# Picking the source of each list place by an exclusive or and a minimum, with the positions added on TensorE

## The chip, the cores and the metric

The kernel runs on one core of one Trainium2 chip. The metric is the device time of one execution in microseconds (us). Three executions of the kernel before took 1736.59, 1736.99 and 1740.82 us.

## The reference

Two layers of graph attention, each followed by a residual and a layer norm, over 3327 nodes with 1024 features. The adjacency is sparse: an edge is drawn with probability 0.0024 in each direction, and every node has its own loop. Cut to what matters:

```python
# layer 0: 8 heads of 128
h = (x @ W).reshape(C, H, D)
e = leaky(alpha_src[:, :, None] + alpha_dst[:, None, :])   # leaky slope 0.2
e = where(adj == 0, -inf, e)
out = softmax(e, -1) @ h
x = layernorm(x + out)
# layer 1: one head of 1024, features after the sum
h = x @ W1
e = leaky(h @ a1 + (h @ a2).T)
x = layernorm(x + relu(softmax(where(adj > 0, e, neg), 1) @ h))
```

## The kernel before

The nodes are cut into 26 tiles of 128 rows (`NT`). The kernel has two arms, by pairs for a dense graph and by lists for a sparse one; these inputs take the lists. It runs in three stages.

**Projection and listing (about the first 580 us).** TensorE multiplies the 26 tiles of x by W0 in fp32 (`together`, L573), with the score columns appended. ScalarE moves the products out (`keep`, L585 to L589), and they are stored as a table of rows `h0_d`. Beside that, a generator `listing` turns the rows of the adjacency into lists of sources, one tile after the other. For each tile:

- `words` (L413, L418) counts ones and packs the mask; `keys` and `columns` (L320, L322, L429 to L444) extract, for every row, up to 32 neighbours as numbers source+1 in a row of `KMAX` = 32 places, `pack`.
- `places` (L462 to L468) writes this list into a moving matrix `mv` in two bf16 parts (high and remainder) and makes a 0/1 matrix `place`, which says for each of 17 x 128 slots to which target row it belongs. `spread` (L474) makes four masked copies of `mv`, one for each group of 32 targets.
- `give` (L486, L493) multiplies `place` by the copies, so that every slot receives its target's list, offset and factors in PSUM. It has three parts (n = 0, 1, 2): the first two hold list, offset and factors, the third only the last bits of the 8 factors (columns `XR:XL`). There are four blocks for the four groups and one of single rows (`EB`).
- `take` (L505 to L512) copies the result out of PSUM on ScalarE.
- `sources` (L520 to L534) picks on VectorE, for each slot, the list entry that it wants: the wanted position is the slot's number less the list's offset, `kq`; a compare of the 32 positions with `kq`, a product with the list and a sum leave source+1, or 0 where the slot is empty. From that comes `idx`, an integer: the row to gather, or a number out of bounds (`NONE`), or row 0 for the four tiles in `FIRST`.

The order on every engine is fixed when the program is built: `pace` is called after every two steps of a projection, and moves `listing`, `counting` and, from tile 13 on, `sums_so_far` ahead by set amounts. `sums_so_far` already gathers rows of `h0_d` by indirect DMAs from GpSimd's queue (L691), weights them on VectorE (L708 to L712) and sums them on TensorE (L721). In VectorE's queue, `sources` of one tile stands right before `places` of the next, and so before its `spread` on ScalarE and its `give` on TensorE.

**Layer 0 by lists (about 581 to 1040 us).** Indirect DMAs gather rows of `h0_d` by `idx` (L1077); VectorE makes weights (L1152 to L1155), TensorE sums (L1178), and the new rows go to `y_d`.

**Layer 1 by lists (about 1040 to 1735 us).** Gathers from `y_d` (L1077), sums (L1278), then the product with W1 (L1310).

`idx` of the last tile ends the first stage: the flag that chooses the arm is read after it, and GpSimd's first instruction of the next stage, L1022, follows it.

Of the kernel before, what the change touches and what calls it, by code (L numbers as in the profile page):

```python
# [12 lines left out]
I32 = mybir.dt.int32  # L13
AF = mybir.ActivationFunctionType
OP = mybir.AluOpType
AX = mybir.AxisListType
# [3 lines left out]
P = 128  # L20
SLOPE = 0.2
EPS = 1e-5
NONE = 1 << 20
# [3 lines left out]
def kernel(  # L27
# [29 lines left out]
    nc = tc.nc  # L57
    N, D = x.shape
    H, DH = a0_src.shape
# [9 lines left out]
    KMAX = 32  # L69
    GT = 32  # L70
    NG = P // GT
    EB = 4
    NB = NG * EB + 1
# [13 lines left out]
    HB = EB // 2  # L87
# [3 lines left out]
    FIRST = 0, 1, EARLY, EARLY + 1  # L91
    XN, XR, XL = 1, 2, 2 + H
    XB = XL + KMAX
    NX, XE = XB + 1, XB + 1
    NY = XE + 2
    XS = 256
    RING = 8
    chunks = [(c, min(CT, NT - c)) for c in range(0, NT, CT)]
    assert NT % 2 == 0 and D == 2 * HALF and DH == P and H * DH == D and w1.shape[1] == D
# [31 lines left out]
    idx = const.tile([P, NT, NB], I32, name="idx")  # L131
# [49 lines left out]
    class Phase:  # L181
# [16 lines left out]
        def sbuf(self, tag, shape, bufs, name=None, dt=F32):  # L198
            return self.pool.tile(shape, dt, tag=tag, name=name or tag, bufs=bufs)
# [66 lines left out]
        def edge_constants(self):  # L266
            self.io_w = self.iota([P, WD], [[1, WD]], "io_w")

            self.io_q = self.iota([P, HG2], [[2 * P, HB], [2, P // 8], [P // 4, 8]], "io_q", base=1)
            self.io_e = self.iota([P, P], [[2, P // 8], [P // 4, 8]], "io_e", base=1)  # L270
            for g in range(1, NG, 2):
                r = slice(g * GT, (g + 1) * GT)
                nc.gpsimd.tensor_scalar(self.io_q[r, :P], self.io_q[r, :P], float(2 * P), None, op0=OP.add)
                nc.gpsimd.tensor_scalar(self.io_q[r, P:], self.io_q[r, P:], float(-2 * P), None, op0=OP.add)
            self.own_g = self.pool.tile([P, NG], F32, bufs=1, name="own_g")
            nc.vector.memset(self.own_g, 0.0)
            for g in range(NG):
                nc.vector.memset(self.own_g[g * GT : (g + 1) * GT, g : g + 1], 1.0)
            part = self.pool.tile([P, 3, NB], I32, bufs=1, name="part")
            nc.gpsimd.iota(part[:, 0, NB - 1 :], pattern=[[0, 1]], base=0, channel_multiplier=1)  # L280
            for b in range(EB):
                for g in range(NG):
                    nc.gpsimd.iota(
                        part[:, 0, b * NG + g : b * NG + g + 1], pattern=[[0, 1]], base=(b + g) % HB * P,
                        channel_multiplier=1,
                    )
            nc.vector.tensor_scalar(
                part[:, 1, :], part[:, 0, :], 7, 4, op0=OP.bitwise_and, op1=OP.logical_shift_left
            )
            nc.vector.tensor_scalar(  # L290
                part[:, 2, :], part[:, 0, :], 3, 15, op0=OP.logical_shift_right, op1=OP.bitwise_and
            )

            nums = self.pool.tile([P, 1], I32, bufs=1, name="nums")
            nc.vector.tensor_scalar(nums, part[:, 0, NB - 1 :], GT - 1, None, op0=OP.bitwise_and)
            self.mvs = self.pool.tile([P, RING, 3, NY], BF16, bufs=1, name="mvs")
            nc.vector.memset(self.mvs, 0.0)
            for c, of in ((XN, nums), (NY - 1, part[:, 0, NB - 1 :])):
                nc.vector.tensor_scalar(
                    self.mvs[:, :, 0, c : c + 1], of.unsqueeze(1).to_broadcast([P, RING, 1]), 1.0, None, op0=OP.add  # L300
                )
            self.places = self.pool.tile([P, RING, 14], F32, bufs=1, name="places")
            self.degrees = self.pool.tile([P, NT, 2], BF16, bufs=1, name="degrees")
            nc.vector.tensor_scalar(part[:, 0, :], part[:, 0, :], -P, None, op0=OP.bitwise_and)
            for n in range(2):
                nc.vector.tensor_tensor(part[:, 0, :], part[:, 0, :], part[:, n + 1, :], OP.bitwise_or)
            self.io_k = self.pool.tile([P, NB], F32, bufs=1, name="io_k")
            nc.vector.tensor_copy(self.io_k, part[:, 0, :])
            self.io_l = self.iota([P, KMAX], [[1, KMAX]], "io_l")
            self.bit = self.pool.tile([P, 8, KMAX], I32, bufs=1, name="bit")  # L310
            self.base = self.pool.tile([P, 8, KMAX], F32, bufs=1, name="base")
            for b in range(8):
                first = (b & 1) * NP // 2 + (b >> 1 & 1) * NP // 4 + (b >> 2) * NP // 8 + 1
                nc.vector.memset(self.bit[:, b, :], 512 << b)
                nc.vector.memset(self.base[:, b, :], float(first))
# [60 lines left out]
    class Edges:  # L376
# [101 lines left out]
        def give(self, b):  # L478

            if b == 0:  # L480
                self.xp = self.ph.xp
            for n in range(3):
                if b == EB:
                    s = slice(XR, XL) if n == 2 else slice(XR, NY)
                    at = NG * NX - XR
                    nc.tensor.matmul(  # L486
                        self.xp[:, EB - 1, at + s.start : at + s.stop], self.place[:, b * P :], self.mv[:, n, s],
                        start=n == 0, stop=n == 2,
                    )
                    continue  # L490
                s = slice(XR, XL) if n == 2 else slice(b // HB, b // HB + XB)
                to = self.xp[:, b, : NG * NX].rearrange("p (g c) -> p g c", g=NG)
                nc.tensor.matmul(  # L493
                    to[:, :, s], self.place[:, b * P : (b + 1) * P], self.mvg[:, :, n, s], start=n == 0, stop=n == 2
                )

        def take(self):
            sbuf = self.ph.sbuf
            self.xs = sbuf("xs", [P, NB, KMAX + 3], 1)
            re = sbuf("re", [P, NB, H], 2)  # L500
            m = NB - 1
            xb = self.xp[:, :, : NG * NX].rearrange("p b (g c) -> p b g c", g=NG)
            xe = self.xp[:, EB - 1, NG * NX :]
            lists = self.xs[:, :m, :].rearrange("p (b g) c -> p b g c", g=NG)
            nc.scalar.activation(lists[:, :, :, 1 : KMAX + 1], xb[:, :, :, XL:XB], AF.Copy)  # L505
            nc.scalar.activation(lists[:, :HB, :, 0], xb[:, :HB, :, 0], AF.Copy)
            nc.scalar.activation(lists[:, HB:, :, 0], xb[:, HB:, :, XB], AF.Copy)
            nc.scalar.activation(self.xs[:, m, 1:], xe[:, H : H + KMAX + 2], AF.Copy)
            nc.scalar.activation(re[:, :m, :].rearrange("p (b g) h -> p b g h", g=NG), xb[:, :, :, XR:XL], AF.Copy)
            nc.scalar.activation(re[:, m, :], xe[:, :H], AF.Copy)  # L510
            nc.scalar.activation(tgt[:, self.t, :m].rearrange("p (b g) -> p b g", g=NG), xb[:, :, :, XN], AF.Copy)
            nc.scalar.activation(tgt[:, self.t, m:], xe[:, NY - 1 - XR : NY - XR], AF.Copy)  # L512
            nc.sync.dma_start(re_d[self.t], re)

        def sources(self):

            sbuf, ph, t = self.ph.sbuf, self.ph, self.t
            xv, m = self.xs, NB - 1
            kq = sbuf("kq", [P, NB], 1)
            nc.vector.tensor_tensor(kq[:, :m], ph.io_k[:, :m], xv[:, :m, 0], OP.subtract)  # L520
            nc.vector.tensor_tensor(kq[:, m:], ph.io_k[:, m:], xv[:, m, KMAX + 2 :], OP.subtract)
            eq = sbuf("eq", [P, NB, KMAX], 1)
            nc.vector.tensor_tensor(
                eq, ph.io_l.unsqueeze(1).to_broadcast([P, NB, KMAX]),
                kq.unsqueeze(2).to_broadcast([P, NB, KMAX]), OP.is_equal,
            )
            nc.vector.tensor_tensor(eq, eq, xv[:, :, 1 : KMAX + 1], OP.mult)
            v = sbuf("v", [P, 2, NB], 1)
            nc.vector.tensor_reduce(v[:, 0, :], eq, AX.X, OP.add)

            nc.vector.tensor_scalar(
                v[:, 1, :], v[:, 0, :], 0.0, float(1 if t in FIRST else NONE), op0=OP.is_equal, op1=OP.mult
            )
            nc.vector.scalar_tensor_tensor(idx[:, t, :], v[:, 0, :], -1.0, v[:, 1, :], op0=OP.add, op1=OP.add)  # L534


    with ExitStack() as own, tc.manual_schedule():
        ph = Phase(own, "proj", {"A": 3})
# [9 lines left out]
        lists = []  # L548
# [373 lines left out]
        for t in range(3, NT):  # L922
# [3 lines left out]
            if t == 5:  # L926
                n, own_a = NT - 1, pool.tile([P, NT], I32, bufs=1, name="own")
                nc.vector.memset(own_a[:, n:], 0)
                step, m = adj.ap[0][0] + 1, rows(n)
# [660 lines left out]
```

## Time and profile before

| what | value |
|---|---|
| executions | 1736.59, 1736.99, 1740.82 us (median 1736.99) |
| the profiled execution's own time | 1737.93 us |
| its span in the profile | 1735.9 us |
| mean granted TensorE clock | 0.923 |
| PE busy | 1461.5 us, 84% |
| DVE (VectorE) busy | 1159.6 us, 67% |
| POOL (GpSimd) busy | 1053.2 us, 61% |
| ACT (ScalarE) busy | 472.7 us, 27% |

The busy shares are means over three stages that differ. They don't say which engine sets the time of the first stage, where the change lies; for that, a table of the busy time in stretches of the span and the waits of each engine in such a stretch are needed. A wait is named by what came last before the waiting instruction.

### The profile page before, as it was taken

The numbers are of one execution on the slowest core, as the hardware profiler recorded it, in microseconds if no ns is written. First come the engines' busy times: TensorE is split into PE (matmuls) and PEld (weight loads), VectorE is DVE, ScalarE is ACT, GpSimd is POOL, SyncE is SP. The second block draws the span as 40 slices with busy tenths as digits, with TensorE's granted clock in tenths as the row PEclk, the third lists the DMA queues.
The fourth block names the chain that finished last, engine by engine and source line by source line (L and its number), as shares of the span: only waits on it lengthen the run. The fifth ranks groups of instructions, "written<-read, shape, count | busy, mean of one in ns | idle before, by whom it ended". The sixth has DMA issues, their size and how long they took to land.

```text
span 1735.9 us, 33973 instructions
## 1 busy us (share of the span) xinstructions
PE 1461.5 (84%) x12635; PEld 840.6 (48%) x12635; DVE 1159.6 (67%) x3132; ACT 472.7 (27%) x1370; POOL 1053.2 (61%) x1311
## 2 busy tenths in 40 slices
PE   9799979889988576567666644999999999999998
PEld 5566655555655355455444432344444444444443
DVE  6699999899997698686877855354444444444443
ACT  5677763333333212222222122110111111110110
POOL 5433245666566576565657666677767776676650
PEclk9899999999999788887888887899999999999999
DMA  7699998999999999999999999999999999999980
GB/s 187 113 166 171 183 247 316 354 399 397 379 361 341 333 409 410 400 399 381 404 389 385 378 387 380 358 399 401 393 395 392 396 392 392 388 393 410 386 332 37
DMA packets 190321, 595.96 MB, mean 343 GB/s; under 512 B 37914, under 2 KB 47924, under 8 KB 190146
## 3 DMA queue, kind: packets, MB, share of 16 engines
q0 software_dynamic: 131056, 459.23, 73.6%
q1 hardware_dynamic: 56052, 123.63, 19.3%
q10 hardware_dynamic: 3038, 10.83, 1.7%
q8 instruction: 102, 1.67, 0.4%
q14 instruction: 73, 0.60, 0.1%
HBM read 593.53 MB, written 54.99 MB: 374 GB/s over the span
## 4 chain that ended last, share of the span: by engine, by line
PE 40%; DMA 12%; DVE 8%; issue 4%; POOL 1%; ACT 0%; DVEq 0%; SPq 0%; ACTq 0%; POOLq 0%
PE mm L1310 22%; PE acc L1278 13%; DMA src<-h_d,idx 4%; DMA near<-h_d,idx 3%; PE acc L1178 3%; DVE e L1155 2%; DMA src<-y_d,idx 1%; DVE y L1195 1%; PE tr L205 1%; DMA own<-h_d 1%; DVE pr L1043 1%; DVE st L226 1%; DMA near<-y_d,idx 1%; DVE y L233 1%; PE acc L1167 1%
## 5 line engine op out<-in xcount | busy, mean ns | idle before, releaser
L573 PE MATMUL mm<-wt,xT 128*128 128x384 f32 (+1 forms) x1248 | 414.3, 477 | 0.5 <-DMA xT<-in_x_t_dram 0.5
L1310 PE MATMUL mm<-wt,xT 128*128 128x512 f32 x832 | 387.6, 605 | 0.0
L1077 POOL DMA_INDIRECT src<-y_d,idx x248 | 252.6, 1019 | 118.9 <-PE acc L1278 43.2
L573 PEld LDWEIGHTS mm<-wt,xT 128*128 128x128 f32 x1248 | 230.3, 194 | 128.3 <-issue 33.5
L1313 DVE SCALAR_TENSOR_TENSOR o<-mm,y 128x512 f32<-128x512 f32 x52 | 36.0, 692 | 315.6 <-PE mm L1310 315.6
L1310 PEld LDWEIGHTS mm<-wt,xT 128*128 128x128 f32 x832 | 149.9, 189 | 198.4 <-issue 193.5
L1077 POOL DMA_INDIRECT src<-h_d,idx x152 | 163.8, 1077 | 86.4 <-PE acc L1178 26.7
L1077 POOL DMA_INDIRECT near<-y_d,idx x168 | 170.5, 1015 | 66.0 <-PE acc L1278 18.2
L691 POOL DMA_INDIRECT near<-h_d,idx x112 | 121.9, 1088 | 65.0 <-PE part L721 36.3
L1178 PE MATMUL acc<-src,e 128*32 128x129 f32 x2432 | 100.7, 333 | 70.8 <-DVE e L1155 70.8
L1278 PE MATMUL acc<-src,es 128*32 128x341 f32 x1488 | 123.2, 465 | 24.3 <-DVE es L1269 24.3
L1077 POOL DMA_INDIRECT near<-h_d,idx x96 | 103.4, 1077 | 61.9 <-PE acc L1178 15.8
L1178 PEld LDWEIGHTS acc<-src,e 128*32 128x32 f32 x2432 | 84.3, 134 | 88.7 <-DVE e L1155 77.6
L1292 ACT ACTIVATE z<-y,ri 128x342 f32<-128x342 f32 (+1 forms) x78 | 39.5, 570 | 298.3 <-DVE ri L1288 298.3
L1178 PE MATMUL acc<-near,e 128*32 128x129 f32 x1664 | 70.9, 340 | 56.1 <-DVE e L1155 45.2
L1155 DVE TENSOR_TENSOR e<-oh,way 128x1024 f32<-128x1024 f32 x90 | 109.9, 1221 | 9.1 <-PE acc L1178 1.0
L208 ACT ACTIVATE xT<-tr 128x512 f32<-128x512 f32 x52 | 31.1, 597 | 236.0 <-PE tr L205 236.0
L1167 PE MATMUL acc<-own,ident 128*128 128x387 f32 (+1 forms) x156 | 70.4, 561 | 29.3 <-ACT own L1137 25.2
L1178 PEld LDWEIGHTS acc<-near,e 128*32 128x32 f32 x1664 | 59.7, 138 | 69.4 <-DVE e L1155 48.7
L1278 PEld LDWEIGHTS acc<-src,es 128*32 128x32 f32 x1488 | 42.7, 111 | 93.7 <-issue 43.0
L413 ACT ACTIVATE junk<-ad 128x1664 uint8<-128x1664 uint8 x52 | 83.0, 1597 | 7.0 <-POOL ad L402 5.4
L1278 PE MATMUL acc<-near,es 128*32 128x342 f32 (+1 forms) x1008 | 82.9, 462 | 2.0 <-DVE es L1269 2.0
(232 smaller groups left out, 2311.1 us busy)
## 6 DMA issues: line engine op xcount, KB each, us to landing
y_d<-y SPq DMA_DIRECT2D x26, 514.0 KB
y<-y_d SPq DMA_DIRECT2D x26, 514.0 KB
xT<-in_x_t_dram SPq DMA_DIRECT2D x26, 512.0 KB
h_d<-ht SPq DMA_DIRECT2D x25, 524.0 KB
y<-in_x_dram SPq DMA_DIRECT2D x25, 512.0 KB
out_dram<-o SPq DMA_DIRECT2D x25, 512.0 KB
ad<-in_adj_dram POOLq DMA_DIRECT2D x25, 415.9 KB
own<-half_d SPq DMA_DIRECT2D x20, 516.0 KB
```

Source lines behind the costliest of these rows:

```text
L208: nc.scalar.activation(part, tr, AF.Copy)
L413: nc.scalar.activation(junk, ad[:, n * THR : (n + 1) * THR], AF.Copy, accum_out=self.d[:, n : n + 1])
L573: nc.tensor.matmul(accs[t, c], xT[t][:, k, :], wt[:, k, CUTS0[c] : CUTS0[c + 1]], start=k == 0, stop=k == KT - 1)
L691: nc.gpsimd.indirect_dma_start(out=src[n % 3][:, g, :], out_offset=None, in_=h0_d[:THR, :], in_offset=bass.IndirectOffsetOnAxis(ap=idx[:, ...
L1077: nc.gpsimd.indirect_dma_start(out=s[:, g, :w], out_offset=None, in_=table[:n, :], in_offset=bass.IndirectOffsetOnAxis(ap=idx[:, t, b * NG ...
L1155: nc.vector.tensor_tensor(e, oh.unsqueeze(2).to_broadcast([P, ng, H, wide]), wp.unsqueeze(3).to_broadcast([P, ng, H, wide]), OP.mult,)
L1167: nc.tensor.matmul(self.acc[n].rearrange("p h d -> p (h d)"), ident, part, start=False, stop=False)
L1178: nc.tensor.matmul(self.acc[h // 3][g * GT : (g + 1) * GT, h % 3, :], e[:, g, h, :], rowsof[:, g, h, :], start=j == 0 and h in HEADS, stop ...
L1278: nc.tensor.matmul(self.acc[c][to, :m], es[:, g, :], s[:, g, CUTS[c] : CUTS[c + 1]], start=b == 0, stop=b == EB,)
L1292: nc.scalar.activation(z[:, cut], self.res[:, cut], AF.Copy, scale=ri[:, 1:2])
L1310: nc.tensor.matmul(acc, xT[:, k, :], wt1[:, k, half], start=k == 0, stop=k == KT - 1)
L1313: nc.vector.scalar_tensor_tensor(o[:, half], acc, 0.0, res[:, half], op0=OP.max, op1=OP.add)
```

## The change

The entries of a list get their position added: entry number l arrives as source+1 plus 4096 l (`STEP` = 4096). TensorE adds it, as the third part of the split: `mv`'s third part holds the 32 numbers 4096 l in the columns of the list, written once for all eight buffers, and the third matmul of every block covers 40 columns of each group in place of 8. `take` writes the lists as int32 in a tile of their own and the offsets in a second one (five copies in place of four). `sources` forms 4096 `kq` as int32, takes the exclusive or of the list with it, which leaves a number under 4096 only at the wanted entry, and takes the minimum over the 32 places.

```diff
+    STEP = 1 << 12
...
-            self.io_l = self.iota([P, KMAX], [[1, KMAX]], "io_l")
+            io_l = self.iota([P, KMAX], [[STEP, KMAX]], "io_l")
+            nc.vector.tensor_copy(self.mvs[:, :, 2, XL:XB], io_l.unsqueeze(1).to_broadcast([P, RING, KMAX]))
...
-                    s = slice(XR, XL) if n == 2 else slice(XR, NY)
+                    s = slice(XR, XB) if n == 2 else slice(XR, NY)
...
-                s = slice(XR, XL) if n == 2 else slice(b // HB, b // HB + XB)
+                s = slice(XR, XB) if n == 2 else slice(b // HB, b // HB + XB)
...
-            self.xs = sbuf("xs", [P, NB, KMAX + 3], 1)
+            self.xs, self.xo = sbuf("xs", [P, NB, KMAX], 1, dt=I32), sbuf("xo", [P, NB], 1)
...
-            nc.scalar.activation(lists[:, :, :, 1 : KMAX + 1], xb[:, :, :, XL:XB], AF.Copy)
-            nc.scalar.activation(lists[:, :HB, :, 0], xb[:, :HB, :, 0], AF.Copy)
-            nc.scalar.activation(lists[:, HB:, :, 0], xb[:, HB:, :, XB], AF.Copy)
-            nc.scalar.activation(self.xs[:, m, 1:], xe[:, H : H + KMAX + 2], AF.Copy)
+            offs = self.xo[:, :m].rearrange("p (b g) -> p b g", g=NG)
+            nc.scalar.activation(lists, xb[:, :, :, XL:XB], AF.Copy)
+            nc.scalar.activation(self.xs[:, m, :], xe[:, H : H + KMAX], AF.Copy)
+            nc.scalar.activation(offs[:, :HB, :], xb[:, :HB, :, 0], AF.Copy)
+            nc.scalar.activation(offs[:, HB:, :], xb[:, HB:, :, XB], AF.Copy)
+            nc.scalar.activation(self.xo[:, m:], xe[:, H + KMAX + 1 : H + KMAX + 2], AF.Copy)
...
-            kq = sbuf("kq", [P, NB], 1)
-            nc.vector.tensor_tensor(kq[:, :m], ph.io_k[:, :m], xv[:, :m, 0], OP.subtract)
-            nc.vector.tensor_tensor(kq[:, m:], ph.io_k[:, m:], xv[:, m, KMAX + 2 :], OP.subtract)
-            eq = sbuf("eq", [P, NB, KMAX], 1)
+            kq, ki = sbuf("kq", [P, NB], 1), sbuf("kqi", [P, NB], 1, dt=I32)
+            nc.vector.tensor_tensor(kq, ph.io_k, self.xo, OP.subtract)
+            nc.vector.tensor_scalar(ki, kq, float(STEP), None, op0=OP.mult)
             nc.vector.tensor_tensor(
-                eq, ph.io_l.unsqueeze(1).to_broadcast([P, NB, KMAX]),
-                kq.unsqueeze(2).to_broadcast([P, NB, KMAX]), OP.is_equal,
+                self.xs, self.xs, ki.unsqueeze(2).to_broadcast([P, NB, KMAX]), OP.bitwise_xor
             )
-            nc.vector.tensor_tensor(eq, eq, xv[:, :, 1 : KMAX + 1], OP.mult)
             v = sbuf("v", [P, 2, NB], 1)
-            nc.vector.tensor_reduce(v[:, 0, :], eq, AX.X, OP.add)
+            nc.vector.tensor_reduce(v[:, 0, :], self.xs, AX.X, OP.min)
+            if t in FIRST:
+                nc.vector.tensor_scalar(v[:, 1, :], v[:, 0, :], float(STEP), None, op0=OP.is_lt)
+                nc.vector.tensor_tensor(v[:, 0, :], v[:, 0, :], v[:, 1, :], OP.mult)
+                nc.vector.tensor_scalar(idx[:, t, :], v[:, 0, :], -1.0, 0.0, op0=OP.add, op1=OP.max)
+                return
...
```

More of the change, by code (lines that the diff above doesn't have):

```diff
@@ L517, in sources @@
             sbuf, ph, t = self.ph.sbuf, self.ph, self.t
-            xv, m = self.xs, NB - 1
-            kq = sbuf("kq", [P, NB], 1)
-            nc.vector.tensor_tensor(kq[:, :m], ph.io_k[:, :m], xv[:, :m, 0], OP.subtract)
-            nc.vector.tensor_tensor(kq[:, m:], ph.io_k[:, m:], xv[:, m, KMAX + 2 :], OP.subtract)
-            eq = sbuf("eq", [P, NB, KMAX], 1)
+            kq, ki = sbuf("kq", [P, NB], 1), sbuf("kqi", [P, NB], 1, dt=I32)
+            nc.vector.tensor_tensor(kq, ph.io_k, self.xo, OP.subtract)
+            nc.vector.tensor_scalar(ki, kq, float(STEP), None, op0=OP.mult)
             nc.vector.tensor_tensor(
-                eq, ph.io_l.unsqueeze(1).to_broadcast([P, NB, KMAX]),
-                kq.unsqueeze(2).to_broadcast([P, NB, KMAX]), OP.is_equal,
+                self.xs, self.xs, ki.unsqueeze(2).to_broadcast([P, NB, KMAX]), OP.bitwise_xor
             )
-            nc.vector.tensor_tensor(eq, eq, xv[:, :, 1 : KMAX + 1], OP.mult)
             v = sbuf("v", [P, 2, NB], 1)
-            nc.vector.tensor_reduce(v[:, 0, :], eq, AX.X, OP.add)
+            nc.vector.tensor_reduce(v[:, 0, :], self.xs, AX.X, OP.min)
[4 more added lines that the diff above has]
+                return
             nc.vector.tensor_scalar(
-                v[:, 1, :], v[:, 0, :], 0.0, float(1 if t in FIRST else NONE), op0=OP.is_equal, op1=OP.mult
+                v[:, 1, :], v[:, 0, :], 0.0, float(NONE), op0=OP.is_equal, op1=OP.mult
             )
```

## The prediction

> **What bounds the kernel now.** The page comes first. Its slices show where VectorE is full:
>
> ```profile
> PE   9799979889988576567666644999999999999998
> DVE  6699999899997698686877855354444444444443
> PEclk9899999999999788887888887899999999999999
> DMA  7699998999999999999999999999999999999980
> ```
>
> One slice is 43.4 us. DVE stands at 9 nearly throughout slices 3 to 12, which is the stage the change lies in, and PE and DMA stand there at 8 or 9 too: three nearly full resources. A table by stages is needed:
>
> ```profile
> core 0: us, PE busy (x) PEld busy (x) DVE busy (x) ACT busy (x) POOL busy (x), PEclk, DMA share, GB/s
> 84.00:120.00 36.00, 34.44 (x147) 22.76 (x146) 33.26 (x96) 25.05 (x72) 13.80 (x57) 1.00 0.95 164
> 120.00:240.00 120.00, 113.64 (x474) 73.27 (x473) 113.40 (x323) 89.09 (x239) 40.12 (x134) 1.00 0.93 163
> 240.00:340.00 100.00, 83.81 (x884) 55.05 (x883) 87.88 (x236) 39.87 (x146) 60.02 (x81) 0.91 0.94 343
> 340.00:500.00 160.00, 146.20 (x1757) 95.90 (x1756) 151.61 (x402) 61.45 (x248) 107.51 (x148) 0.99 1.00 384
> 500.00:581.00 81.00, 66.72 (x752) 42.64 (x750) 58.45 (x154) 26.43 (x106) 43.56 (x50) 0.90 0.94 349
> 581.00:1040.00 459.00, 286.97 (x4494) 220.26 (x4494) 350.27 (x867) 96.48 (x212) 299.85 (x279) 0.80 1.01 391
> ```
>
> From 120 to 240 us DVE is busy 113.40 us with 323 instructions. The missing 6.6 us are 20 ns behind each of them, the step from one DVE instruction to the next that the timeline shows everywhere. So it never stands still; its waits in that stretch are an empty list. PE, at 113.64 us, waits 6.4 us:
>
> ```profile
> L493 PE MATMUL xp<-mvg,place 128*128 128x168 bf16 x59 | 9.3, 238 | 6.4 <-ACT mvg L474 6.4
> ```
>
> L474 in turn waits for DVE's L463. From 340 to 500 us DVE is again full (151.61 us, and 402 gaps of 20 ns are 8.0), with 0.7 us of waits. There PE waits for DVE, in weights (L712: 5.9 us) and sums (L754: 5.1 us). So **VectorE sets the pace from 120 to 240 and from 340 to 500 us**, with PE some 5% behind it and the DMA engines close. From 240 to 340 and from 500 to 581 us DVE waits too:
>
> ```profile
> DVE w L708 <- DMA near<-h_d,idx: 6.6, 4, 4.1
> DVE ad L754 <- PE part L721: 5.1, 3, 2.1
> DVE kq L520 <- ACT xs L507: 4.5, 2, 3.3
> ```
>
> These are 500 to 581 us, in total, times and longest; from 240 to 340 it waits 5.5 us for near and 1.7 us for L750. After 581 us the change touches nothing.
>
> **The change part by part.** What goes and stays on DVE:
>
> ```profile
> L527 DVE TENSOR_TENSOR eq<-eq,xs 128x544 f32<-128x544 f32 x26 | 19.0, 730 | 0.9
> L523 DVE TENSOR_TENSOR eq<-io_l,kq 128x544 f32<-128x544 f32 x26 | 18.9, 725 | 0.9
> L529 DVE TENSOR_REDUCE v<-eq 128x17 f32<-128x544 f32 x26 | 18.8, 722 | 0.9
> L441 DVE TENSOR_TENSOR bits<-ki,bit 128x256 int32<-128x256 int32 x26 | 10.9, 419 | 0.0
> L443 DVE TENSOR_TENSOR cols<-ki,base 128x256 f32<-128x256 int32 x26 | 10.9, 419 | 0.0
> L439 DVE TENSOR_SCALAR ki<-ki 128x32 int32<-128x32 int32 x26 | 4.7, 182 | 0.9
> ```
>
> *Removed per tile:* the compare L523, which takes 0.76 us from its start to the next one's, and the second subtraction L521, 0.18. *Added:* one small tensor_scalar (4096 kq), 0.21 by the step from L531 to L534. *Exchanged:* the product L527 for the exclusive or, the sum for the minimum, both still over 544 elements. No row has an exclusive or or an integer reduce. The nearest are L441, int32 bitwise, and L443, int32 in and fp32 out, at 419 ns each, so neither integers nor the bit operation cost anything; I take the old durations. If the integer reduce ran at half rate it would cost 0.57 us more and leave 0.16 of the saving; if both did, nothing.
>
> [...] The exclusive or reads 4096 kq once per 32 columns with step 0. [...] But L523 has that same broadcast as second source and takes 725. [...]
>
> So an ordinary tile saves 0.76 + 0.18 - 0.21 = 0.73 us of DVE. The four tiles of FIRST get one small tensor_tensor more, 0.21, and save 0.52. 22 x 0.73 + 4 x 0.52 = 18.1 us. The single copy into mvs has 256 elements, 0.3 us as the CAST io_q of that size. **DVE loses 17.8 us.**
>
> *PE:* the third matmul of a block goes from 32 to 160 columns.
>
> ```profile
> L493 PE MATMUL xp<-mvg,place 128*128 128x168 bf16 x208 | 32.8, 241 | 20.5 <-ACT mvg L474 18.9 <-ACT cnt L367 1.2 <-ACT places L346 0.4
> L493 PE MATMUL xp<-mvg,place 128*128 128x32 bf16 x104 | 18.9, 182 | 0.0
> ```
>
> (241 - 182)/136 is 0.43 ns per column, so 128 columns cost 0.055 us, and the 32 of the single block 0.014. 4 x 0.055 + 0.014 is 0.23 us per tile, 6.1 us over 26. The lower bound is nothing, since the next weight load (98 ns) may cover it. I take it whole; it lies in PE's idle time, and where that is gone, it counts.
>
> *ACT:* one more copy of one element, like L512's 246 ns, and kq now waits for the last of five copies. DVE reaches kq 0.6 to 5.0 us after ACT's L508 in tiles 2 to 23, so this is covered; in tiles 0, 1, 24 and 25 DVE waits for ACT, and it costs up to 0.2 us. Int32 output of ACT has no row here; L505 moves 512 fp32 in 0.61, taken as it is, with up to its double (0.6 us) under the same slack. What stands behind kq on DVE is places, for which spread and give wait, so a late kq would reach PE. No DMA, SP or POOL instruction is added or moved, and the order on every engine stays.
>
> *What arrives at the end,* by stages:
> - 84 to 240 us: 10 tiles. DVE gives 0.5 (tile 0's is lost in the wait of tile 1) + 8 x 0.73 = 6.4. PE's idle time is 1.6 + 6.4 = 8.0, less 10 x 0.23: 5.7. With two engines level, not all of it is had: 4.5.
> - 240 to 340: four tiles, 2.9. The fourth's (313.6 us) runs into the 4.9 us wait for a gather at 321: 2.2, of which I take 1.8.
> - 340 to 500: eight tiles, 5.4 (two are in FIRST). PE has 13.8 us free. The DMA engines show a share of 1.00 where the gather stage, 581 to 1040 us, has 1.01; a faster DVE frees gather buffers sooner, but transfers may then be late. Half: 2.7.
> - 500 to 581: DVE waits 18.6 us anyway. Only the last tile's sources end the stage, the direct 0.5 us; with something from the others 1.0.
>
> Sum 10.0 us. The next two stages start earlier and last as long. Against the profiled execution, 1737.9 - 10.0 = 1727.9; it lay 0.9 above the median of the runs, so 1727.
>
> **The rivals.**
> - *DVE's saving comes through nearly whole* (13 to 18 us). For: no waits on DVE for 280 us. Against: PE's idle time after its new columns. 1719 to 1724.
> - *The DMA engines take over from 240 us on,* and only the first 156 us gain: 3 to 5 us, 1732 to 1734. For: shares of 0.94 to 1.00 and 8.6 us of waits for gathers at the end. Against: 0.4 us of such waits from 340 to 500.
> - *TensorE becomes the bound (slower).* Place: L493 between the projections. If PE's time counts now, and its idle 5% is only a shadow of the trace's modelled ends, the 6.1 us are added and DVE's saving buys nothing: 1743. It decides as soon as PE's waits for L474 are not real standstill. Against: 20 us of named waits there.
> - *The change doesn't do what it says:* integer forms at half rate on DVE or ACT eat the saving. 1735 to 1739.
>
> **How the numbers follow.** Partial gain (5 to 13 us) 0.45; nearly whole 0.22; DMA takes over 0.16; TensorE 0.10; integer forms 0.07. About 0.3%, 5.2 us, is what a measurement of this kernel can tell from no change. Faster by more: 0.45 + 0.22 and a little of the third, 0.70. Within: most of the third and half of the last, 0.17. Slower: 0.13. The range runs from the whole saving, 1719, to just above no change, 1738; the likeliest case alone has 1724 to 1732.
>
> **What would show it.** Right: L527's successor at 0.73 us and the integer minimum at 0.72; DVE still without waits from 120 to 240 us, with the seven tiles there about 0.5 us closer; the 160-column matmul near 0.24; L1022 about 10 us earlier than 580.45; the stretch behind it as long as before. Wrong: kq waiting for ACT in most tiles, PE without idle time there, more waits for near and far than 5.5 + 8.6 us, or L1022 not earlier.

## The result, and the profile after

The changed kernel takes 1731.43 us in the median of 9 runs (1726.90 to 1735.24), the kernel before 1736.99 in 9 (1734.63 to 1740.82). The ratio is 0.9969, 95% interval 0.9959 to 0.9979. In the last of the comparisons below it was 0.9956 (0.9940 to 0.9972), 1730.02 against 1737.01 us. So the change makes the kernel a little faster, by 5.6 and 7.0 us or 0.3 to 0.4%. The forecast was 1727, a gain of 10, with 1719 to 1738 as its range. Three slow executions (1980.6, 2030.1 and 3587.2 us) are left out of the medians and counts below.

The table by stages of the changed kernel, to be read beside that of before (cut at 577 and 1035 us, where its stages turn):

```profile
core 0: us, PE busy (x) PEld busy (x) DVE busy (x) ACT busy (x) POOL busy (x), PEclk, DMA share, GB/s
84.00:120.00 36.00, 35.06 (x149) 23.37 (x149) 32.77 (x98) 26.22 (x82) 13.32 (x56) 1.00 0.95 157
120.00:240.00 120.00, 116.81 (x487) 75.78 (x486) 111.02 (x322) 91.67 (x248) 40.70 (x136) 1.00 0.95 170
240.00:340.00 100.00, 87.16 (x949) 56.21 (x948) 88.88 (x242) 41.70 (x163) 62.37 (x86) 0.95 0.97 364
340.00:500.00 160.00, 143.63 (x1709) 94.31 (x1711) 146.36 (x393) 61.93 (x257) 109.55 (x148) 0.98 1.00 383
500.00:577.00 77.00, 66.14 (x730) 41.66 (x719) 51.18 (x137) 23.12 (x94) 40.18 (x46) 0.90 0.93 335
577.00:1035.00 458.00, 292.39 (x4494) 224.37 (x4494) 349.74 (x869) 96.49 (x212) 297.65 (x278) 0.80 1.01 392
```

From 120 to 240 us PE went from 113.64 to 116.81 us busy: it stands still for 3.2 us there where it stood 6.4, and is now as full as VectorE. From 340 to 500 us VectorE fell from 151.61 to 146.36 us, and the DMA share is 1.00 and the rate 383 GB/s (384 before). VectorE now stands still where it did not. These were its waits in that stretch in the kernel before (rows: what waited for what, in total, times, longest):

```profile
DVE w L708 <- DMA near<-h_d,idx: 0.4, 1, 0.4
DVE ad L754 <- ACT ad L750: 0.3, 1, 0.3
```

and these are the ones in the changed kernel:

```profile
DVE w L713 <- DMA near<-h_d,idx: 4.1, 6, 1.1
DVE w L713 <- DMA far<-h_d,idx: 1.5, 1, 1.5
```

Seven times in that stretch the weights now wait for a gathered row. And from 84 to 240 us VectorE, which from 120 on had never stood still, has these:

```profile
DVE kq L523 <- ACT xo L512: 6.7, 3, 4.7
DVE io_t L264 <- POOL junk L262: 1.2, 1, 1.2
```

Of the 6.7 us, 5.7 lie in the first two tiles, where the kernel before waited 5.2 us in the same way. The other 1.0 us, after 120 us, is new: VectorE now comes to `kq` before ScalarE has copied the offsets. So is the 1.2 us wait for a number pattern from GpSimd.

The groups of the first stage that the change made (each row is a line and shape, with its count, busy us, mean ns and idle time before it; rows between them are left out where marked):

```profile
L525 DVE TENSOR_TENSOR xs<-xs,kqi 128x544 int32<-128x544 int32 x26 | 18.9, 728 | 0.9
L529 DVE TENSOR_REDUCE v<-xs 128x17 f32<-128x544 int32 x26 | 18.8, 721 | 0.9
...
L524 DVE TENSOR_SCALAR kqi<-kq 128x17 int32<-128x17 f32 x26 | 5.0, 194 | 0.9
...
L523 DVE TENSOR_TENSOR kq<-io_k,xo 128x17 f32<-128x17 f32 x26 | 4.5, 172 | 11.5 <-ACT xo L512 11.5
...
L495 PE MATMUL xp<-mvg,place 128*128 128x168 bf16 x208 | 32.9, 241 | 13.1 <-ACT mvg L476 10.9 <-DVE top L322 1.3 <-ACT cnt L369 0.9
L495 PE MATMUL xp<-mvg,place 128*128 128x160 bf16 x104 | 24.6, 237 | 0.0
...
L508 ACT ACTIVATE xs<-xp 128x512 int32<-128x512 f32 x26 | 15.5, 597 | 68.6 <-PE xp L488 68.6
```

The exclusive or takes 728 ns and the integer minimum 721, as the fp32 product (730) and sum (722) did; ScalarE writes int32 in 597 ns, where fp32 took 607. The widened matmul takes 237 where the narrow one took 182. So the prices that the prediction put on the single instructions hold. What has to be looked at is how much of VectorE's saving arrives.

To see where, the starts of the reduction over the 32 places (L529) of tiles 0, 10, 14, 21 and 25 cut the first stage in four. Times in us between these starts, from the timelines (differences are taken before rounding):

| kernel | tile 0 to 10 | 10 to 14 | 14 to 21 | 21 to 25 |
|---|---|---|---|---|
| before | 166.3 | 90.9 | 142.8 | 94.0 |
| changed | 163.0 | 87.0 | 143.3 | 94.4 |
| less work on VectorE (the prediction's 0.73 and 0.52 us per tile) | 7.1 | 2.9 | 4.9 | 2.7 |
| arrived | 3.2 | 4.0 | -0.5 | -0.4 |

Up to tile 14 (335 us) 7.2 of about 10 us arrive; behind it nothing does. Layer 0, from its first gather of h_d to the first of y_d, takes 452.9 us before and 453.0 after; layer 1, from there to the end of the span, 700.5 and 699.5. So in this pair of traces nearly the whole gain is made in the first stage, and before 340 us. More traces, below, change this picture in part.

### The profile page after: what moved, and what is told of

The parts are those of the page before. It is cut to its first block, busy times and chain, and to the rows that moved or that the text cites. A ratio compares the mean times of both kernels' runs of the same rounds, so it can differ in the third digit from the quotient of the medians.

```text
span 1729.6 us, 33978 instructions
## 1 busy us (share of the span) xinstructions
PE 1469.5 (85%) x12635; PEld 845.5 (49%) x12635; DVE 1144.2 (66%) x3111; ACT 474.6 (27%) x1396; POOL 1050.5 (61%) x1311
## 3 DMA queue, kind: packets, MB, share of 16 engines
q1 hardware_dynamic: 56052, 123.63, 19.3%
## 4 chain that ended last, share of the span: by engine, by line
PE 40%; DMA 15%; DVE 7%; issue 3%; POOL 1%; ACT 0%; DVEq 0%; ACTq 0%; POOLq 0%; SPq 0%
PE mm L1315 22%; PE acc L1283 13%; DMA src<-h_d,idx 6%; PE acc L1183 3%; DMA near<-h_d,idx 2%; DVE e L1160 2%; DMA own<-half_d 2%; PE tr L206 1%; DMA near<-y_d,idx 1%; DMA src<-y_d,idx 1%; DMA end<-h_d,idx 1%; DVE y L1200 1%; DVE pr L1048 1%; PE acc L1172 1%; DMA own<-h_d 1%
## 5 line engine op out<-in xcount | busy, mean ns | idle before, releaser
L696 POOL DMA_INDIRECT near<-h_d,idx x112 | 123.2, 1100 | 60.5 <-PE part L726 30.6
L1082 POOL DMA_INDIRECT near<-h_d,idx x96 | 106.0, 1104 | 65.5 <-PE acc L1183 12.5
```

What stands on the lines that cost most here:

```text
L696: nc.gpsimd.indirect_dma_start(out=src[n % 3][:, g, :], out_offset=None, in_=h0_d[:THR, :], in_offset=bass.IndirectOffsetOnAxis(ap=idx[:, ...
L1082: nc.gpsimd.indirect_dma_start(out=s[:, g, :w], out_offset=None, in_=table[:n, :], in_offset=bass.IndirectOffsetOnAxis(ap=idx[:, t, b * NG ...
```

## The experiments

Three theories for the missing part. **A/D:** from about 340 us on, the gathers' transfers are so close behind VectorE that a faster VectorE waits for them. **B/E:** TensorE's wider matmuls, or something else that is not bytes, took it. **C:** VectorE's work is not what the time hangs on. Ratios are against the kernel before in the same comparison. In the comparison of the next four experiments the changed kernel itself did not run, so they meet it only through its ratios, 0.9969 and 0.9956, from the two others.

**TensorE's part alone.** The kernel before with the wide third matmul, whose new columns hold zeros:

```diff
-                s = slice(XR, XL) if n == 2 else slice(b // HB, b // HB + XB)
+                s = slice(XR, XB) if n == 2 else slice(b // HB, b // HB + XB)
```

(and the same for the block `EB`). Expected:

> The kernel before with the third matmul of every block widened to 40 columns of each group (what is added is zero, so the sums stay as they were); nothing else of the change. It prices the added TensorE work alone, 6.1 us if all of it counted. Theory A (VectorE sets the pace to about 340 us and transfers take over behind it; TensorE's columns lie in its idle time): 0 to 2 us over before, 1737 to 1739. Theory B (the part of the saving that did not arrive was eaten by TensorE's wider matmuls): 4 to 6 us over before, 1741 to 1743.

Measured: 1739.11 us (13 runs) against 1737.23 (33); ratio 1.0010 (1.0001 to 1.0019), 1.7 us. TensorE's 6.1 us of new work are mostly hidden, as A has it; B's 4 to 6 us are outside the interval.

**The saving without TensorE's part.** The changed kernel with the positions added to `pack` on VectorE; two bf16 parts then hold the sum, and the third matmul is narrow again:

```diff
+            nc.vector.tensor_tensor(pack, pack, ph.io_l, OP.add)
             nc.vector.tensor_copy(mv[:, 0, XL:XB], pack)
...
-                s = slice(XR, XB) if n == 2 else slice(b // HB, b // HB + XB)
+                s = slice(XR, XL) if n == 2 else slice(b // HB, b // HB + XB)
```

> The changed kernel with the positions added to the list on VectorE (one add of 32 elements per tile, about 0.21 us with its step) ahead of the split, which two bf16 parts then hold; the third matmul is narrow as before. VectorE's saving falls from 17.8 to about 12 us, TensorE's 6.1 us are gone. Theory A: within 1.5 us of the changed kernel, since the late stretch waits for transfers and the early one loses on VectorE what it wins on TensorE: 1730 to 1733. Theory B: 3 to 5 us faster than the changed kernel, 1726 to 1728.

Measured: 1732.02 us; ratio 0.9966 (0.9953 to 0.9979), not to be told from the changed kernel. Sparing TensorE 6.1 us and giving VectorE 5.5 back come to nothing together, as A has it: the first is worth about 1.7 us by the experiment before, and the second about as much if a third to a half of VectorE's work counts. B's 1726 to 1728 did not come.

**The saving undone.** The changed kernel with one more exclusive or of 544 elements per tile, 19.8 us in all:

```diff
+            pad = sbuf("pad", [P, NB, KMAX], 1, dt=I32)
+            nc.vector.tensor_tensor(pad, self.xs, ki.unsqueeze(2).to_broadcast([P, NB, KMAX]), OP.bitwise_xor)
```

> The changed kernel with one more exclusive or over 544 elements per tile on VectorE into a tile that nothing reads: 0.76 us per tile, 19.8 us in all, which puts VectorE's work back to that of before while TensorE keeps the wide matmul. Theory A: the slope of VectorE's work is about a third of it, so it loses the whole gain and lands at 1736 to 1739. Theory B: 4 to 6 us over before, 1741 to 1743. Theory C (VectorE's work hardly matters, the gain came from something else in the change, such as fewer instructions or copies): 1731 to 1733.

Measured: 1739.28 us (22 runs); ratio 1.0012 (1.0003 to 1.0021). That is where the wide matmul alone stands (1.0010). With VectorE's work put back, everything else in the change brings no gain, which rules out C. From the changed kernel's 0.9969 and 0.9956 to 1.0012 it is 0.43 to 0.56%, 7.5 to 9.7 us for 19.8 us of VectorE's work: some 0.4 to 0.5 of it counts, a little more than the third that was expected.

**A little more of the same.** The changed kernel with the offsets multiplied by 4096 in ScalarE's copy, and copied first, so that the tensor_scalar L524 goes:

```diff
-            nc.scalar.activation(offs[:, :HB, :], xb[:, :HB, :, 0], AF.Copy)
+            nc.scalar.activation(offs[:, :HB, :], xb[:, :HB, :, 0], AF.Copy, scale=up)
...
-            nc.vector.tensor_tensor(kq, ph.io_k, self.xo, OP.subtract)
-            nc.vector.tensor_scalar(ki, kq, float(STEP), None, op0=OP.mult)
+            nc.vector.tensor_tensor(ki, ph.io_k, self.xo, OP.subtract)
```

> The changed kernel with the offsets copied first by ScalarE and already multiplied by 4096 there, so that one VectorE subtraction gives the int32 number and the tensor_scalar behind it goes: 0.21 us per tile, 5.5 us of VectorE in all, and where VectorE waits for ScalarE (7 us in 84 to 240 us in the changed kernel) it can start up to 0.5 us earlier. Theory A: 1 to 3 us faster than the changed kernel, 1728.5 to 1730.5, all of it won before 340 us. Theory B (TensorE is the bound now): no change, 1731 to 1732.

Measured: 1729.06 us; ratio 0.9950 (0.9934 to 0.9966). It is faster than the kernel before; against the changed kernel the intervals overlap, so the expected 1 to 3 us are neither shown nor excluded.

**Bytes out of the way, first try.** Half of each row gathered in the first stage, from the fourth buffer on:

```diff
-                        out=src[n % 3][:, g, :], out_offset=None, in_=h0_d[:THR, :],
+                        out=src[n % 3][:, g, : HG if n < 3 else HG // 2], out_offset=None, in_=h0_d[:THR, :],
```

on the kernel before, on the changed kernel, and on the one with the positions added on VectorE; beside them the scaled offsets with the memsets of the gather buffers' ends moved from GpSimd to VectorE (`nc.vector.memset(end, 0.0)`).

> The kernel before; from its fourth buffer on, every gather of sums_so_far (L691) fetches only the first half of each row, so the sums of the first stage work on partly old data. Instructions, their order and all other engines' work are the same; about 42 MB of 230 MB of the first stage's gathers and later ones go. Theory D (transfers absorb VectorE's saving from 340 us on): VectorE still fills 340 to 500 us here, so little is won there; the 14 us of waits for near and far outside of it shrink: 1725 to 1732. Theory E (the late stretch is held by TensorE or GpSimd's issue, not by the bytes): 1735 to 1738.

> The changed kernel with the same halved gathers in the first stage (part of the data left out). To be read against the kernel before with halved gathers. Theory D: with the bytes out of the way, VectorE's 17.8 us arrive much more fully: 10 to 15 us faster than that one. Theory E: the difference stays at 5 to 7 us, as with whole gathers.

> The changed kernel with halved gathers and, besides, the positions added on VectorE with the third matmul narrow (VectorE saves about 12 in place of 17.8 us, TensorE nothing added). If VectorE alone is the bound once the bytes are gone: about 5 us slower than the changed kernel with halved gathers. If TensorE is then the bound: 2 to 5 us faster than it.

> The changed kernel with the offsets scaled and copied first by ScalarE (as before in that experiment), and the two memsets of the gather buffers' ends at the turn of the stages (L1027, 1.88 us on GpSimd ahead of its first gather) on VectorE, which stands still there. If GpSimd's first gather sets the start of the next stage: another 1 to 2 us faster than with scaled offsets alone, 1727 to 1728. If its release or the next stage's transfers hide it: 1729.

Measured: 1783.96, 1765.89, 1775.32 and 1767.77 us, against 1766.60 (25 runs) for the kernel before on that chip: it runs this kernel 30 us slower than the others did. Ratios 1.0097 (1.0074 to 1.0121), 0.9991 (0.9973 to 1.0010), 1.0040 (1.0021 to 1.0060) and 1.0005 (0.9990 to 1.0019). No theory had the first at 17 us *more*. PE's waits from 340 to 500 us in the last of the four show what is different there:

```profile
PE part L726 <- issue: 10.6, 26, 2.7
PE xp L495 <- issue: 1.8, 3, 0.9
```

"issue" is standstill that no other engine or transfer in the profile accounts for, so why TensorE stands before its small sums is not known; that it waits there for its own instructions, as is said in the expectations below, was the author's reading, and no trace shows it. This comparison therefore does not answer the question. Of the three with halved gathers, the changed kernel is 18.1 us faster than the kernel before and 9.4 us faster than the one with the positions on VectorE. The order fits "VectorE alone is the bound once the bytes are gone", but both differences are larger than expected, and from 340 to 500 us VectorE waits there for ScalarE's offsets for 9.0 us in the changed kernel. What moving the memsets brings can't be told: the scaled offsets alone were not run on that chip, and GpSimd's first gather waited there for ScalarE's L1031 (8.86 us of standstill before it) in place of its own memsets.

**Bytes out of the way, second try**, with both unhalved kernels beside the halved ones, so that all four traces come from the same chip:

> The kernel before, unchanged, for its trace on the chip of this comparison; the second comparison ran on a chip where the same kernel took 1766.6 in place of 1737 us, with TensorE waiting for its own instructions between the small matmuls (10.6 to 11.7 us of such waits from 340 to 500 us, none in the first traces). Every theory: the same as the runs of before. If its trace shows those waits again, the late stretch here is held by TensorE's instructions and says nothing about transfers; if not, the four runs can be read as the second comparison was meant.

> The changed kernel, unchanged. On a chip without those waits 5 to 7 us faster than before. Where they are there, theory D (transfers) expects the same 5 to 7, theory F (the gain depends on what holds TensorE in the late stretch) anything from 0 to 15.

> The kernel before with the halved gathers of the first stage (from its fourth buffer on each row's first half only; the sums work on partly old data). Without the instruction waits theory D expects 0 to 10 us less than before; on the other chip it was 17 us more, which no theory expected; if that comes back here without them, halving itself costs something and the pair must be read against each other alone.

> The changed kernel with the same halved gathers (part of the data left out). Theory D: 10 to 17 us faster than the kernel before with halved gathers, on any chip, because VectorE's 17.8 us arrive once no transfer is late. Theory E (something other than bytes holds the late stretch): 5 to 7 us.

| kernel | us (median) | ratio to the kernel before | 95% interval |
|---|---|---|---|
| before | 1738.63 | 1.0005 | 0.9992 to 1.0019 |
| changed | 1730.02 | 0.9956 | 0.9940 to 0.9972 |
| before, half rows | 1723.54 | 0.9918 | 0.9897 to 0.9938 |
| changed, half rows | 1710.54 | 0.9849 | 0.9829 to 0.9868 |

The kernel before, with whole rows, has no "issue" among PE's waits from 340 to 500 us on this chip; its first two are

```profile
PE part L721 <- DVE e L712: 5.8, 6, 1.5
PE part L721 <- DVE ad L754: 5.4, 3, 4.2
```

so the four can be read as meant. In medians the change gains 7.0 us with whole rows (1737.01 to 1730.02) and 13.0 with half rows (1723.54 to 1710.54); in means it is 8.0 and 11.7. Worked out by resampling the single runs, the 95% interval of the difference between the two gains is about 0.1 to 6.9 us (means): the direction is theory D's, the size is hardly known. The kernel before was expected to lose up to 10 us by halving; it lost 13.5. The stretch from 340 to 500 us follows for each of the four, with the columns of the table by stages. The kernel before:

```profile
340.00:500.00 160.00, 145.31 (x1754) 95.41 (x1752) 149.88 (x397) 62.34 (x251) 107.96 (x148) 0.99 0.99 378
```

The changed kernel:

```profile
340.00:500.00 160.00, 144.14 (x1738) 94.45 (x1740) 148.12 (x396) 62.19 (x259) 109.03 (x151) 1.00 1.01 389
```

The kernel before with half rows:

```profile
340.00:500.00 160.00, 145.12 (x1728) 94.86 (x1726) 152.01 (x407) 63.29 (x256) 112.27 (x147) 0.99 0.78 253
```

The changed kernel with half rows:

```profile
340.00:500.00 160.00, 148.42 (x1765) 96.89 (x1764) 151.77 (x407) 63.99 (x265) 111.82 (x152) 0.99 0.80 259
```

The DMA share falls from 0.99 and 1.01 to 0.78 and 0.80, and VectorE is full in both halved kernels (152 us and 407 steps of 20 ns on the mean make the 160). Its list of waits in this stretch is empty in both. With whole rows the kernel before waits for a gather there once,

```profile
DVE w L708 <- DMA far<-h_d,idx: 1.4, 1, 1.4
```

and the changed kernel six times:

```profile
DVE w L713 <- DMA near<-h_d,idx: 2.6, 4, 1.0
DVE w L713 <- DMA far<-h_d,idx: 0.8, 2, 0.6
```

The experiments left more traces, and together they tell more than one pair does. Four with whole rows have about as much work on VectorE as the kernel before, four have less of it (positions on VectorE 12, scaled offsets 23 in place of 17.8 us, by the sums above). Cut by tiles as above, in us:

| trace | tile 0 to 10 | 10 to 14 | 14 to 21 | 21 to 25 | waits for near and far, 340 to 500 us |
|---|---|---|---|---|---|
| before | 166.3 | 90.9 | 142.8 | 94.0 | 0.4 |
| before, last comparison | 167.7 | 90.8 | 143.8 | 93.7 | 1.4 |
| wide matmul alone | 168.4 | 90.7 | 143.4 | 94.4 | 1.2 |
| saving undone | 167.9 | 90.6 | 143.4 | 94.9 | 0.6 |
| changed | 163.0 | 87.0 | 143.3 | 94.4 | 5.6 |
| changed, last comparison | 162.8 | 88.6 | 141.2 | 92.4 | 3.4 |
| positions on VectorE | 163.3 | 87.7 | 142.4 | 93.3 | 3.0 |
| scaled offsets | 162.1 | 87.8 | 141.9 | 92.9 | 6.7 |
| **saved, mean of four against four** | 4.8 | 3.0 | 1.1 | 1.0 | 3.8 longer |
| before, half rows | 167.8 | 88.1 | 141.7 | 85.2 | none |
| changed, half rows | 162.7 | 84.1 | 138.0 | 84.8 | none |
| **saved, half rows** | 5.1 | 4.0 | 3.7 | 0.4 | |

Before tile 10, where these gathers have hardly begun, halving changes nothing. From tile 14 to 21 VectorE has about 4.9 us less to do and 1.1 arrive; in all four traces with less work on VectorE the waits for gathered rows are longer (3.0 to 6.7 us) than in any of the four others (0.4 to 1.4), and with half the bytes they are gone. That is what theory D says, and for this stretch it is shown: a part of VectorE's saving turns into waiting for transfers. How much more arrives with half rows rests on one pair of traces. In the last stretch halving helps both kernels (94.2 to 85.2 and 93.3 to 84.8 us), so there the transfers were late in the kernel before already; the change gains little even with half rows. VectorE waits there in the halved changed kernel for the offsets from ScalarE (7.2 us) and for TensorE's sums (4.6 us).

Up to the last tile the four traces with less work are 9.9 us shorter, and their first gather of layer 0 comes 8.7 us earlier. Over the whole span 7.1 us are left: layer 0 takes as long in both (453.1 and 452.8 us), but layer 1 takes 697.9 to 700.7 us in the first four and 699.5 to 703.5 in the others. The ranges overlap, and why layer 1 should be longer was not tested. The same scatter stands in the half rows' pair, where layer 1 is 3.5 us shorter in the changed kernel, so the 13.0 and 7.0 us above are not a matter of the first stage alone.

## Why the prediction was right

It forecast faster, at 1727 with 1719 to 1738; 1731.4 came, and 1730.0 in the last comparison. By its steps:

- **VectorE sets the pace.** Shown by undoing the saving: the whole gain goes with it.
- **17.8 us of VectorE's time.** The compare's 18.9 us are gone and the subtractions take 4.5 in place of 8.7; 5.0 came for the product with 4096, 0.7 for the four tiles of FIRST, 0.3 for the copy. That is 17.1 us less busy, and 21 instructions fewer with a step of 34 ns each are 0.7 more: 17.8. (The page's total, 1159.6 before and 1144.2 after, falls by 15.4 only; instructions outside the change took 1.7 us longer in that trace.) The "20 ns behind each" of the prediction is a mean: from 120 to 240 us in the kernel before, 174 of the 300 steps that the timeline shows between VectorE instructions are gaps of about 34 ns, and in nearly all the others the next instruction starts before the end of the one before. That it never stood still is right all the same.
- **No integer form and no broadcast costs more.** The exclusive or takes 728 ns over 544 columns with 4096 `kq` read at step 0; the compare L523, with the same broadcast, took 725. The integer minimum takes 721, where the fp32 sum took 722. The 0.57 us that the prediction puts on an integer reduce at half rate is what two rows of before give as an estimate: 722 ns for 544 columns in L529 and 419 for 256 in L441 are 1.05 ns per column, 0.57 us over 544. A minimum at half rate would by that estimate have taken about 1290 ns.
- **TensorE +6.1 us, in its idle time.** The price was 55 ns per matmul, as forecast (237 less 182). Of it 1.7 us show when nothing is saved on VectorE; PE's idle time from 120 to 240 us shrank from 6.4 to 3.2 us and was not used up.
- **84 to 240 us: 4.5 us.** 4.8 came in the mean of the traces. Right; that VectorE and TensorE are level there is what the busy times of 120 to 240 us show.
- **240 to 340: 1.8 us.** 3.0 came. Too low: the wait for the gather at 321 us is as long as before (waits for near in the stretch are 3.9 to 5.4 us, where they were 4.2 to 5.5), so the gather came earlier together with what stood ahead of it.
- **340 to 500: half of 5.4 us, 2.7.** 1.1 came in the mean, over seven of the eight tiles (-0.5 and 2.6 in the two pairs of the kernels themselves). This term was too high. The reason for the half, late transfers, was right; the DMA share of 1.00 deserved more weight than VectorE's nearly empty list of waits, which said only that the transfers were *just* in time.
- **500 to 581: 1.0 us.** 1.0 came, but not by the direct 0.5 us of the last tile: `idx` does not end the stage, though the prediction and the account of the kernel before say so. The flag is written earlier (at 575.76 us in the kernel before, where the last `idx` starts at 579.95). In the trace of the wide matmul alone GpSimd's first instruction of the next stage starts before the last `idx` (start, duration, instruction, idle time before):

```profile
582.97 1.91 POOL L1022 MEMSET end<- 128x1048 f32 x2 [7.28 <-DMA h_d<-ht]
584.01 0.18 DVE L534 SCALAR_TENSOR_TENSOR idx<-v 128x17 int32<-128x17 f32 x1
```

  The profile names landings of stores (of h, of re, of half_d) as what released it, another one from trace to trace (of h after 7.93 us of standstill in the kernel before, of re after 7.16 in the changed kernel); which of them sets the turn was not tested.
- **The sum.** 10.0 us were forecast for the first stage and 9.9 came up to the last tile. That it closes so well is partly luck: one term was too low by about as much as another was too high. The 5.6 and 7.0 us of the whole kernel are less than that, and the step that does not hold to the end is "the next two stages start earlier and last as long": 8.7 us arrive at their start and 7.1 at the end of the span in the traces, with layer 1 as the open part.

Of the signs that the prediction named, those on single instructions came (728, 721 and 237 ns). L1022's successor starts 5.3 us earlier in the first pair and 11.6 in the last, around the forecast 10. One sign of "right" failed: VectorE waits 2.2 us from 120 to 240 us. One sign of "wrong" came in part: waits for near and far from 240 us to the last tile are 19.3 us in the changed kernel's first trace, over the 14.1 named, but 15.9 against 15.6 in the last comparison.

Of the rivals, "the DMA engines take over from 240 us on" came true in a milder form and from about 340 us; it gave 1732 to 1734, and the median lies just under that.

## What to carry to other kernels

VectorE, without waits from 120 to 240 us, set the pace here, but what the saving on it brought was bounded by the next resource, and its own list of waits (0.7 us from 340 to 500 us) did not show how near that was. So look at the idle time of the second engine and at the DMA share in the same stretch before counting a saving in full. Here 17.8 us off the leading engine bought about 10 in its stage and 5.6 to 7.0 in the kernel, because TensorE was 5% behind it in one stretch (113.64 us busy of 120) and the transfers had less room than that in another (a DMA share of 1.00). To test whether transfers are the next bound, take bytes away on both kernels, before and after, and see whether the new waits go; a difference of two differences of whole times is weak evidence when each time scatters by 2 to 3 us. And cut every trace at hand at the same places before trusting one pair: the first pair alone said that nothing arrives behind tile 14.

## What was not expected of the hardware

One chip ran the same kernel in 1766.6 in place of 1737 us. In the traces from there TensorE stands before small matmuls without a releaser in the profile, 8.1 to 11.7 us between 340 and 500 us where the two traces of the kernel before in other comparisons have none. Layer 1 took 726 to 731 us in place of 698 to 704, which is most of the 30 us, though the granted clock there was no lower (0.94 in place of 0.92). There, halving the gathers made the kernel before 17 us slower, where it made it 13.5 us faster on another chip. What holds TensorE there was not found.
